# One small GpSimd write behind every row gather of a graph kernel's third pass

## The chip, the cores and the metric

The kernel runs on one core of one Trainium2 chip. The metric is the device time of one execution in microseconds (us), as the median of several timed runs. A profile is one further execution, recorded by the hardware profiler; its time stands beside its span below.

## The reference

Two graph layers follow each other over 12500 nodes with 64 features each and 400000 edges, whose edges are sorted by destination. The first layer takes a mean over the source nodes of each node's edges, twice, with tanh. The second layer is the one that the change lies in. For each edge it makes a gate from the edge's 64 attributes, multiplies it with the row of the edge's source node, and sums the products by destination node:

```python
def ssp(x):
    return jax.nn.softplus(x) - LOG2
h = node_feats_in @ Wn.T + bn
h_src = h[src]                                   # a row of 64 floats per edge
w = ssp(edge_feats @ We1.T + be1)
w = ssp(w @ We2.T + be2)
m = h_src * w
agg = jax.ops.segment_sum(m, dst, num_segments=V)
out = ssp(agg @ Wc.T + bc)
return out @ Wp.T + bp
```

Each layer ends with a residual addition and a layer norm.

## The kernel before

Three passes over the edges follow each other. Passes one and two serve the first layer (one-hot matrices that are counted, kept in HBM and used again, with gathers on line 438). A short stage then makes the rows `h` of the second layer and stores them in HBM as `t3`, 64 floats a node. Pass three, `edge_pass(second, message_pools)`, is the second layer's edge work.

Pass three works in 391 groups (NG = 390 and a shorter last one). A group is T = 8 columns of 128 edges, 1024 edges. The body stands in a hardware loop over `windows`, which runs once for these inputs; the 391 groups are written out inside it, and a scheduler orders the instructions of each engine by their dependencies.

- `Group.gather` (line 866) fills a tile `got` of 128 x 8 x 64 floats with eight indirect DMAs on GpSimd's queue (line 870), one per column of 128 edges: each reads 128 row numbers from `srcs` and fetches 128 rows of `t3`. There are eight `got` buffers, so the gathers may run eight groups ahead of the product that reads them. Completion is counted on eight semaphores in turn, so a gather also waits for the landing of the gather eight before it.
- `second` is a software pipeline of three stages: in step k it starts group k (gather, load of the attributes `att` on SP's queue at line 948, transposes `m_t` on TensorE, copy `m_at` on ScalarE, first layer at line 971), advances group k - 1 (second layer at line 965, logarithms on ScalarE at lines 932 and 933) and finishes group k - 2.
- Finishing a group is: transposes `m_b` (line 958), the product `m_m` = gate x `got` on VectorE (line 961), eight matmuls with the one-hot tile `same` into `p_sum` (line 885), and the addition of `p_sum` into a window of `acc` on VectorE (line 903, `Group.place`).

`m_m` is what waits for the eight gathers of its group, and its end is what frees the `got` buffer for the group eight later. GpSimd has no other work in pass three than the 3125 gathers and one MEMSET of `att` (line 947) in the short last group.

Of the kernel before, what the change touches and what calls it, by code (L numbers as in the profile page):

```python
# [9 lines left out]
F32 = mybir.dt.float32  # L10
# [9 lines left out]
P = 128  # L20
# [47 lines left out]
def gnn_kernel(ctx, tc, x, src, dst, ea, W_lin, b_lin, W1_agg, W1_root, b1, W2_agg, W2_root, b2,  # L68
               Wn, bn, We1, be1, We2, be2, Wc, bc, Wp, bp, out):
    nc = tc.nc  # L70
# [239 lines left out]
    def across(row, shape):  # L310
        return row.unsqueeze(1).to_broadcast(shape)
# [527 lines left out]
    big = ctx.enter_context(tc.tile_pool(name="big", bufs=1))  # L839
    cps = ctx.enter_context(tc.tile_pool(name="cps", bufs=1, space=PSUM))  # L840
    acc = big.tile([F, NA], F32, name="acc")
    base = big.tile([P, NG + 1], F32, name="base")
    base_i = big.tile([1, NG + 1], I32, name="base_i")
    steps = cps.tile([P, 512], F32, name="steps")
    nc.vector.tensor_copy(steps[:, :W], ramp[:, :W])
    e_att = ea[:NG * ET, :].rearrange("(g p t) f -> g p t f", p=P, t=T)
# [2 lines left out]
    def edge_pass(stages, pools):  # L849

        nc.vector.memset(acc, 0.0)
        nc.vector.tensor_copy(base, first)
        with ExitStack() as st:
            sb = st.enter_context(tc.tile_pool(name="esb", bufs=3))
            ps = st.enter_context(tc.tile_pool(name="eps", bufs=2, space=PSUM))
            work = pools(st)
            at = {}

            class Group:
                def __init__(self, g):
                    self.g, self.n = g, T if g < NG else TL
                    self.got = None

                def gather(self):
                    self.got = sb.tile([P, T, F], F32, name="got", bufs=8)
                    for t in range(self.n):
                        c = self.g * T + t
                        nc.gpsimd.indirect_dma_start(  # L870
                            out=self.got[:, t, :], out_offset=None, in_=t3[:, :],
                            in_offset=bass.IndirectOffsetOnAxis(ap=srcs[:, c:c + 1], axis=0))

                def compare(self):
                    n = self.n
                    self.same = sb.tile([P, T, W], F32, name="same")
                    nc.vector.tensor_tensor(  # L877
                        self.same[:, :n, :], across(steps[:, :W], [P, n, W]),
                        rel[:, self.g * T:self.g * T + n].unsqueeze(2).to_broadcast([P, n, W]),
                        op=ALU.is_equal)  # L880

                def gathered_sum(self, m):
                    self.p = ps.tile([F, W], F32, name="p_sum")
                    for t in range(self.n):
                        nc.tensor.matmul(self.p, m[:, t, :], self.same[:, t, :],  # L885
                                         start=t == 0, stop=t == self.n - 1)

                def place(self):
                    g = self.g
                    if g % 8 == 0:  # L890
                        k = min(8, NG + 1 - g)
                        loads, v = nc.values_load_multi_w_load_instructions(
                            base_i[0:1, g:g + k], engines=(mybir.EngineType.DVE,), min_val=0, max_val=NP,
                            skip_runtime_bounds_check_because="a base is a node's number, held at NP or "
                            "less where it moves, and acc has W columns more", bass_reorder=False)
                        at.update({g + i: v[i] for i in range(k)})
                        if g:
                            for load in loads:
                                tc.add_manual_dep(load.ins, at["last"].ins.name, mybir.DependencyInfo(
                                    mybir.DependencyClass.NoSync, mybir.DependencyReason.DATA),  # L900
                                    reason="in order")
                    here = acc[:, ds(at[g], W)]
                    at["last"] = nc.vector.tensor_tensor(here, self.p, here, op=ALU.add)  # L903

            with tc.For_i(0, windows, 1):
                nc.vector.tensor_copy(base_i, base[0:1, :])
                stages(work, [Group(g) for g in range(NG + 1)])
                nc.vector.tensor_scalar(base, base, float(W), float(NP), op0=ALU.add, op1=ALU.min)
                nc.vector.tensor_scalar(rel, rel, -float(W), None, op0=ALU.add)
# [13 lines left out]
    def second(work, groups):  # L923
# [15 lines left out]
        for k in range(len(groups) + 2):  # L939
# [38 lines left out]
            if old:  # L978
                old.gathered_sum(old.m)
                old.place()  # L980

    edge_pass(second, message_pools)


# [70 lines left out]
```

## Time and profile before

| | us |
|---|---|
| median of 3 timed runs | 6985.22 (6981.7 to 6987.38) |
| the profiled execution | 8350.39 |
| its span, first to last instruction | 8348.6 |
| first gather of pass three, last `acc` of it | 3376.3, 8216.9 |
| mean granted TensorE clock of the profiled execution | 0.760 |

The profiled execution is 1365 us longer than the median of the timed runs. Places in the profile are given in microseconds from the start of the span. In the rows of the profile, POOL is GpSimd, DVE is VectorE, ACT is ScalarE and PE is TensorE; a group of instructions is named by its line, engine and operation and by its output and input tiles, and the text behind an arrow names what ended the wait before it. "issue" is idle time for which nothing recorded was waited for; "remote" is a wait whose releaser the profile does not know.

### The profile page before, as it was taken

What the parts mean: (1) busy time and instruction counts of PE and PEld (TensorE: products, weight loads), DVE (VectorE), ACT (ScalarE), POOL (GpSimd) and SP (SyncE); (2) the same over time, 40 slices, a digit from 0 to 9 for tenths busy, and PEclk for the clock granted to TensorE, in tenths of its full rate; (3) what the DMA queues carried; (4) which work ended last, traced back from release to release, by engine and by line L of the source; (5) the groups of instructions that cost most, each with busy time, mean ns of one, the idle gap of its engine ahead of it and who ended that gap; (6) DMA issues with size and microseconds to landing.
All of it is one profiled execution on the core that took longest, in us unless ns stands there. A gap on an engine that the chain in (4) does not pass through costs nothing.

```text
span 8348.6 us, 77646 instructions
## 1 busy us (share of the span) xinstructions
PE 4576.7 (55%) x27549; PEld 2560.1 (31%) x27549; DVE 3612.9 (43%) x5716; ACT 2669.7 (32%) x4067; POOL 4837.1 (58%) x4741
## 2 busy tenths in 40 slices
PE   2788888853444445355445455544554554454555
PEld 1344444421221224233223233323332332232333
DVE  3687788751111114343434344434444443443335
ACT  1788888850000001122222222222222222222224
POOL 1676767626555551566666566666666666666660
PEclk9899999876666666677777777777777777777776
DMA  2565555565665675112111122221211211111110
GB/s 55 188 236 225 215 227 225 220 258 190 237 260 221 260 265 172 46 43 44 43 43 44 41 45 44 45 43 43 43 44 44 44 43 42 43 45 41 44 43 20
DMA packets 364128, 933.43 MB, mean 112 GB/s; under 512 B 135808, under 2 KB 167904, under 8 KB 363518
## 3 DMA queue, kind: packets, MB, share of 16 engines
q1 hardware_dynamic: 191951, 787.41, 25.2%
q0 software_dynamic: 151744, 131.99, 8.9%
q10 hardware_dynamic: 20015, 8.71, 0.5%
q8 instruction: 232, 3.80, 0.2%
q14 instruction: 186, 1.52, 0.1%
HBM read 581.70 MB, written 346.02 MB: 111 GB/s over the span
## 4 chain that ended last, share of the span: by engine, by line
another core or an unknown queue 20%; PE 14%; issue 10%; DVE 8%; ACT 3%; POOL 3%; DMA 2%; DVEq 1%; POOLq 0%; ACTq 0%; SPq 0%
PE m L965 5%; PE m L971 3%; POOL got L870 3%; PE p_sum L885 3%; DVE m_v L936 2%; DMA got<-t,srcs 2%; DVE m_m L961 1%; DVE same L877 1%; ACT m_w L932 1%; ACT m_at L954 1%; DVE m_w L928 1%; ACT m_w L933 1%; DVE m_v L928 1%; PE m_b L958 1%
## 5 line engine op out<-in xcount | busy, mean ns | idle before, releaser
L870 POOL DMA_INDIRECT got<-t,srcs x3125 | 2968.6, 950 | 2023.9 <-DVE m_m L961 924.1
L438 POOL DMA_INDIRECT got<-sent,gidx x1578 | 1818.8, 1153 | 1265.9 <-PE p_got L449 503.8
L965 PE MATMUL m<-m_v,we 128*128 128x512 f32 x782 | 626.6, 894 | 1991.2 <-DVE m_v L936 1714.5
L530 ACT CAST counts<-p_counts 128x784 bf16<-128x784 f32 x1664 | 1284.0, 821 | 249.7 <-PE p_counts L528 134.4
L932 ACT ACTIVATE m_w<-m_w 128x512 f32<-128x512 f32 x391 | 246.9, 631 | 3035.2 <-DVE m_w L928 2626.5
L528 PE MATMUL p_counts<-to,lo 128*128 128x392 bf16 x3328 | 882.6, 355 | 216.6 <-ACT counts L530 145.2
L885 PEld LDWEIGHTS p_sum<-same,m_m 128*64 128x64 f32 x6250 | 776.5, 153 | 535.1 <-DVE m_w L928 233.1
L885 PE MATMUL p_sum<-same,m_m 128*64 128x128 f32 x6250 | 872.9, 299 | 94.5 <-DVE m_m L961 93.0
L903 DVE TENSOR_TENSOR acc<-p_sum,acc 64x128 f32 x391 | 110.1, 282 | 1829.1 <-remote 1634.5
L515 DVE TENSOR_TENSOR to<-ramp,keys 128x1568 bf16<-128x1568 f16 x832 | 797.3, 971 | 156.9 <-PE p_counts L528 95.4
L965 PEld LDWEIGHTS m<-m_v,we 128*128 128x128 f32 x782 | 156.1, 249 | 2079.1 <-DVE m_v L936 1776.7
L674 PE MATMUL p_sums<-counts,addends 128*64 128x512 bf16 x2548 | 460.4, 463 | 237.4 <-issue 192.3
L971 PE MATMUL m<-m_at,we 128*128 128x512 f32 x782 | 570.4, 822 | 0.7 <-ACT m_at L954 0.7
L537 PE MATMUL p_sums<-counts,addends 128*64 128x256 bf16 x5096 | 487.0, 286 | 8.2 <-ACT counts L530 4.3
L877 DVE TENSOR_TENSOR same<-steps,rel 128x1024 f32<-128x1024 f32 x391 | 471.4, 1206 | 0.0
L528 PEld LDWEIGHTS <-lo 128*128 128x128 bf16 x3328 | 263.4, 102 | 586.6 <-issue 483.0
L961 DVE TENSOR_TENSOR m_m<-m_b,got 128x512 f32<-128x512 f32 x391 | 267.3, 684 | 369.9 <-remote 160.3
L681 ACT COPY rs<-p_sums 128x512 f32<-128x512 f32 x26 | 15.2, 586 | 1257.6 <-remote 1020.3
L954 ACT COPY m_at<-m_t 128x512 f32<-128x512 f32 x391 | 225.4, 576 | 595.8 <-PE m L971 481.3
L936 DVE SCALAR_TENSOR_TENSOR m_w<-m,be_c,m_w 128x512 f32<-128x512 f32 x391 | 292.7, 749 | 268.3 <-ACT m_w L933 149.9
L958 PE MATMUL m_b<-ident,m_w 128*128 128x128 f32 x1564 | 248.8, 283 | 288.4 <-DVE m_w L936 173.7
L553 DVE TENSOR_TENSOR v_rest<-misc,parts 128x68 f32<-128x68 f32 x52 | 11.8, 227 | 911.5 <-ACT parts L550 908.8
(263 smaller groups left out, 5191.4 us busy)
## 6 DMA issues: line engine op xcount, KB each, us to landing
kept<-counts SPq DMA_DIRECT2D x364, 896.0 KB
counts<-kept SPq DMA_DIRECT2D x364, 896.0 KB
att<-in_edge_attr_dram SPq DMA_DIRECT2D x390, 256.0 KB
got<-t,srcs POOLq DMA_INDIRECT x3125
got<-sent,gidx POOLq DMA_INDIRECT x1578
t<-h SPq DMA_DIRECT2D x7, 448.0 KB
xs<-in_x_dram ACTq DMA_DIRECT2D x6, 448.0 KB
xs<-in_x_dram SPq DMA_DIRECT2D x6, 448.0 KB
```

What stands on the lines that cost most here:

```text
L438: nc.gpsimd.indirect_dma_start(out=got[i][:, t, :], out_offset=None, in_=sent[step][:, :], in_offset=bass.IndirectOffsetOnAxis(ap=gidx[:, ...
L515: nc.vector.tensor_tensor(t.rearrange("p n (j two) -> p n j two", two=2), ramp[:, :width].rearrange("p (j two) -> p j two", two=2).unsquee ...
L528: nc.tensor.matmul(p[:, k, :MW], made["lo"][:, q % 4 * 2 + k, :], made["to"][:, q % 2 * 2 + k, :], start=True, stop=True)
L530: nc.scalar.copy(counts[:, :, q * 2 * DW:(q + 1) * 2 * DW].rearrange("p h (k d) -> p h k d", k=2), p[:, :, :MW].rearrange("p k (d h) -> p ...
L537: nc.tensor.matmul(p[r:r + YW, :HI * DW], addends[:, h, :], counts[:, h - of, :], start=h < 2, stop=h >= NPP - 2)
L674: nc.tensor.matmul(p[r:r + YW, :], addends[:, h, :], counts[:, :, j, :], start=h < 2, stop=h >= NPP - 2)
L870: nc.gpsimd.indirect_dma_start(out=self.got[:, t, :], out_offset=None, in_=t3[:, :], in_offset=bass.IndirectOffsetOnAxis(ap=srcs[:, c:c + ...
L877: nc.vector.tensor_tensor(self.same[:, :n, :], across(steps[:, :W], [P, n, W]), rel[:, self.g * T:self.g * T + n].unsqueeze(2).to_broadcas ...
L885: nc.tensor.matmul(self.p, m[:, t, :], self.same[:, t, :], start=t == 0, stop=t == self.n - 1)
L936: nc.vector.scalar_tensor_tensor(a, p, bias, a, op0=ALU.add, op1=ALU.max)
L965: nc.tensor.matmul(mid.p2, we2, mid.v, start=True, stop=True)
L971: nc.tensor.matmul(new.p1, we1, at, start=True, stop=True)
```

## The change

A tile `apart` of 128 x 1 floats is made beside `acc`, and behind every indirect DMA of `Group.gather` the source has one GpSimd MEMSET of zeros to it. Nothing reads the tile. Lines below line 843 move down by one or two.

```diff
     base_i = big.tile([1, NG + 1], I32, name="base_i")
+    apart = big.tile([P, 1], F32, name="apart")
     steps = cps.tile([P, 512], F32, name="steps")
...
                         nc.gpsimd.indirect_dma_start(
                             out=self.got[:, t, :], out_offset=None, in_=t3[:, :],
                             in_offset=bass.IndirectOffsetOnAxis(ap=srcs[:, c:c + 1], axis=0))
+                        nc.gpsimd.memset(apart, 0.0)
```

## The prediction

> **What bounds the kernel now.** I read the page's busy times and slices first, to find pass three; then the waits inside it; then the timelines of GpSimd and of VectorE, because the change touches one instruction stream alone.
>
> ```profile
> POOL 1676767626555551566666566666666666666660
> ...
> L870 POOL DMA_INDIRECT got<-t,srcs x3125 | 2968.6, 950 | 2023.9 <-DVE m_m L961 924.1
> ```
>
> The first is GpSimd's row of the page's 40 slices, the second a group of the page. The gathers of pass three (line 870) start at 3376.3 us, the last `acc` update is at 8216.9 us: pass three has 4841 us of the 8348.6 us span. 3125 gathers keep GpSimd busy for 2969 us at about 0.95 us each, and no slice of GpSimd is full. The waits of 3700 to 8200 us say why (total, times, longest):
>
> ```profile
> DVE acc L903 <- remote: 1535.1, 172, 13.5
> POOL got L870 <- DVE m_m L961: 877.1, 206, 7.3
> POOL got L870 <- issue: 764.3, 2491, 1.3
> ```
>
> Third row: nearly every gather begins about 0.30 us after the one before has ended, with nothing to wait for. So a gather costs 0.947 + 0.304 = 1.251 us from start to start, 10.0 us for a group of eight, and 3125 x 1.251 = 3909 us for the pass if nothing holds it up. Second row: in the profiled execution GpSimd also stands still for a `got` buffer, which `m_m` of eight groups earlier frees; it is the faster side there. First row: what holds the compute side is a stall of VectorE before `acc` that nothing recorded explains. In VectorE's timeline:
>
> ```profile
> 5013.13 0.28 DVE L903 TENSOR_TENSOR acc<-p_sum,acc 64x128 f32 x1 [11.62 <-remote]
> ...
> 5023.16 0.28 DVE L903 TENSOR_TENSOR acc<-p_sum,acc 64x128 f32 x1 [2.10 <-PE m_b L958]
> ...
> 5030.67 0.27 DVE L903 TENSOR_TENSOR acc<-p_sum,acc 64x128 f32 x1
> ```
>
> Without the stall one group takes 5030.67 - 5023.16 = 7.5 us of compute; with the stalls the mean is 4841 / 391 = 12.4 us. GpSimd's 10.0 us lie between.
>
> The timed runs decide which side counts. The profiled execution took 8350.39 us (span 8348.6, so 2 us around it), the median of the timed runs is 6985.22: 1365 us less. If pass three ran at GpSimd's pace there, it would save 4841 - 3909 = 932 us, and 433 would come from the 3376 us before it. If the stalls stayed, the whole 1365 us would have to come from those 3376, 40% of them, though TensorE is 82 to 87% busy from 200 to 1700 us (409 to 434 us of each 500 in the table of stretches). So I take the stall to belong to the profiled execution and the gathers, at 10.0 us a group against 7.5 of compute, to bound pass three in the timed runs. That is inferred, not seen.
>
> **The change part by part.** It adds 3125 writes of zero to a 128x1 tile, one in the source behind each gather; it removes nothing. In the changed program the streams of TensorE, VectorE, ScalarE and SP hold the same instructions in the same order with the same waits. Only GpSimd's differs, and not as the words say. Each write waits for the completion of the write before it (same tile, GpSimd's own semaphore), and for nothing else; the scheduler pulls the writes ahead of gathers that still wait for a buffer. The order is: 120 gathers (groups 0 to 14) with one write between any two; then 113 groups with 14 to 35 writes in a row ahead of each, mostly 25, none inside a group; then the last 2101 gathers with no write at all. In all 119 + 14 + 14 x 35 + 14 x 27 + 84 x 25 + 24 = 3125, so 3006 stand in rows.
>
> What one write costs. The trace has these on GpSimd:
>
> ```profile
> 0.25 0.10 POOL L1044 MEMSET const-float32-0.0<- 128x1 f32 x1 [0.25 <-issue]
> 0.28 0.10 POOL L1044 MEMSET const-float32-1.0<- 128x1 f32 x1
> 0.30 0.11 POOL L1044 MEMSET const-bfloat16-1.0<- 128x1 bf16 x1
> 0.33 0.12 POOL L1044 MEMSET const-uint8-127<- 128x1 uint8 x1
> 0.74 0.20 POOL masks.py:197 MEMSET ident<- 128x128 f32 x1 [0.29 <-POOLq L1044]
> ```
>
> ```profile
> 8154.50 0.95 POOL L870 DMA_INDIRECT got<-t,srcs  x1 [0.30 <-issue]
> 8155.49 0.53 POOL L947 MEMSET att<- 128x512 f32 x1
> 8156.65 0.95 POOL L870 DMA_INDIRECT got<-t,srcs  x1 [0.64 <-DVE m_m L961]
> 8157.91 0.95 POOL L870 DMA_INDIRECT got<-t,srcs  x1 [0.30 <-issue]
> ```
>
> A 128x1 write takes 0.10 us, 128x128 takes 0.20, 128x512 takes 0.53 even straight behind a gather: 0.10 fixed and 0.83 ns an element. So mixing gathers and writes makes neither longer; the 0.64 us before the next gather is put down to `m_m`, which ends at 8156.38, and the usual 0.27 us from there to a gather's start is the rest.
>
> For 3006 writes in rows two readings compete. The rows: the four constants wait for nothing and end at 0.35, 0.38, 0.42 and 0.45 us, 0.035 us apart, because the next is under way before the one ahead has completed. The Trainium skill (Perfetto Trace Analysis, section GPSIMD Engine Instruction) advises just that measure: distrust the reported span on GpSimd and use the spacing of consecutive instructions. It would price the rows at 3006 x 0.035 = 105 us. But those four have no wait between them, and the new writes have one each: completion has to be signalled first. GPSIMD Engine Reference, section Instruction dispatch, draws that line: completion does not hold back the next Pool instruction, only what waits for the semaphore. So I take the full 0.10 us, plus the 0.03 us that a single wait on an engine's own semaphore costs (0.01 from end to signal for the `ident` write, about 0.02 from signal to start on VectorE and ScalarE): 0.13 us. No chain of small GpSimd writes is in the trace; the ends I keep are 0.035 below and 0.25 above (twice the value, if the wait costs as much again as the write).
>
> Sum for the timed runs: rows 3006 x 0.13 = 391 us. Between single gathers the wait is long over; a write costs between 0.035 and 0.14 us (0.04 to its start plus 0.10), 119 x 0.09 = 11 us. Together 402 us, all on GpSimd, which I hold to be the bound: in groups 15 to 127 it needs 10.0 + 26.6 x 0.13 = 13.5 us a group against 7.5. Behind GpSimd's writes are queued the next group's gathers; who waits for them is `m_m` (line 961), then `p_sum` and `acc`. The buffer lead of eight groups covers nothing there, since a slower GpSimd has no lead. The `att` loads on SP, the port to SBUF (0.5 KB a write) and the extra 200 KB of instruction code are costed at nothing: GpSimd's own 13.5 us a group covers them, and as `att` is 256 KB a group already loaded in 7.5 to 12 us, a loss there would be below 1 us a group.
>
> Against the profiled execution's own 8350.39 us the sum is smaller: at 12.4 us a group GpSimd has slack, so groups 15 to 127 pay 113 x (13.5 - 12.4) = 123 us, less up to eight groups of lead (about 80 us): 8390 to 8475 us, if its stalls recur as before.
>
> **The rivals.** (A) GpSimd bounds the timed pass: 6985 + 402 = 7387; with 0.11 to 0.18 us a write, 7325 to 7545. For: the arithmetic of the 1365 us. Against: in the one execution that can be seen, it waits for buffers.
>
> (B) The stalls are partly real in the timed runs, and slack hides part of the writes. At 11.3 us a group, halfway, the 113 groups pay 113 x (13.5 - 11.3) = 249 us, less 80 of lead: about 7155. For: the 206 waits for `m_m`. Against: 1365 us can't be found then.
>
> (C) The wait on the own semaphore is as good as free and writes pass at 0.035 us: 105 + 4 = 109 us, 7094.
>
> (D) The other side: faster. Many stalls end 2.5 to 4 us after GpSimd's last gather, when it has run out of buffers (last gather at 4011.13 us, `acc` at 4015.08); a pause in the gathers may be what releases TensorE. The rows of writes are such a pause in front of each of 113 groups. It pays only if the timed pass is stall-bound (say 11.3 us a group) and GpSimd stays under that, so from below (11.3 - 10.0) / 26.6 = 0.049 us a write; at 0.035 it gives 113 x (11.3 - 10.9) = 45 us, 6940.
>
> (E) The change doesn't do what it says: that much is certain for 3006 of 3125 writes. Its effect is in (A); were all of it hidden, 6985.
>
> **How the numbers follow.** A 0.65, B 0.14, C 0.05, a write near 0.25 us (3006 x 0.25 = 750 us, about 7740) 0.07, E hidden 0.03, D 0.06. The time given is A's, rounded to 7385. The range has A's (up to 7545) and goes down to 7110, which takes in B and leaves out C, D and E below and the dearest writes above, some 2 in 10. Faster is D, 0.06; same is E, 0.03; slower is the rest, 0.91. About 0.2% (14 us) is what a measurement of this kernel can tell from no change.
>
> **What would show it right or wrong.** Right: about 26 MEMSETs of `apart` in a row ahead of each group from about the 121st gather on, starting 0.13 us apart; gathers still 0.947 us long and 1.251 apart inside a group; GpSimd's waits for `m_m` gone in groups 15 to 127 and back after them. Wrong: writes starting 0.035 or 0.25 us apart; a gather behind a write longer than 0.95 us, or starting more than 0.30 us after it; stalls before `acc` that go away in the groups with rows; a timed loss far below 300 us, which would say that GpSimd was not the bound of the timed pass.

## The result and the profile after

The changed kernel takes 7502.28 us (median of 4 runs, 7496.97 to 7508.05) against 6986.3 us (the three runs before and one more, 6981.7 to 6995.71): a ratio of 1.0737, 95% interval 1.0718 to 1.0755, or 516 us more. The forecast was 7385 us in a range of 7110 to 7545.

The profile of before that the prediction was read from belongs to a disturbed execution, 20% above every timed run (what disturbed it is not known); when the same kernel was profiled again, as the run before_again, that execution took 6984.9 us (span 6983.1), and after's profiled one took 7496.97 (span 7495.1). These two are compared here. First the undisturbed profile of before: GpSimd's slices, the shares of the chain that ended last, and the group of the gathers (busy us, mean ns | idle us ahead, most of it).

```profile
POOL 0787777772777774277777777777777777777771
...
POOL 32%; DMA 13%; issue 11%; PE 2%; DVE 1%; ACT 1%; POOLq 0%; another core or an unknown queue 0%; DVEq 0%; ACTq 0%; SPq 0%
...
L870 POOL DMA_INDIRECT got<-t,srcs x3125 | 2963.0, 948 | 1150.8 <-issue 839.2
```

GpSimd stands at 7 tenths through all of pass three (0.945 us of each 1.249), the chain runs through it and its transfers, and the idle time ahead of the gathers is "issue", no longer `m_m`. The waits of pass three (2917 to 6857 us; total, times, longest) say who waits for whom:

```profile
DVE m_m L961 <- DMA got<-t,srcs: 1520.4, 384, 5.0
...
POOL got L870 <- issue: 839.2, 2755, 0.3
```

VectorE waits for the gathers in 384 of 391 groups. GpSimd starts nearly every gather 0.3 us after the one before has ended, and no wait of its own for `m_m` is left. So the prediction's inference holds: pass three runs at GpSimd's pace. Now after, the same rows of its page, with the writes:

```profile
POOL 0877777736777743777677767777777777777771
...
L871 POOL DMA_INDIRECT got<-t,srcs x3125 | 2961.1, 948 | 1174.6 <-issue 898.4
...
L874 POOL MEMSET apart<- 128x1 f32 x3125 | 311.2, 100 | 167.2
```

The gathers have kept their length (948 ns). The writes hold the engine for only 311 us, with 167 us idle ahead of them. Three stretches of after's pass three show where the time went: lone writes, then rows of writes, then none.

```profile
core 0: us, PE busy (x) PEld busy (x) DVE busy (x) ACT busy (x) POOL busy (x), PEclk, DMA share, GB/s
2924.00:3090.00 166.00, 103.21 (x432) 64.19 (x433) 87.62 (x114) 47.67 (x81) 141.07 (x254) 0.81 0.25 59
3090.00:4718.00 1628.00, 807.00 (x3170) 585.73 (x3169) 546.44 (x792) 339.31 (x568) 1148.27 (x3897) 0.73 0.17 37
4718.00:7341.00 2623.00, 1692.43 (x7244) 1100.79 (x7242) 1237.05 (x1812) 773.38 (x1293) 1982.72 (x2102) 0.82 0.24 52
```

Only the middle stretch differs: 113 groups in 1628 us, 14.4 us each, where before takes 9.99. TensorE is half busy there and its granted clock drops to 0.73, but it is not what holds the groups up: `m_m` waits for the gathers in all 113 of them, 894 us in total, and TensorE's sums into `p_sum` wait for `m_m` as often. The last stretch has before's pace (1.2485 us from gather to gather). From the first to the last gather pass three takes 4415.2 us against 3914.2: 501 of the 512 us between the two spans. Another 8 lie ahead of the pass and 3 behind it; both are left unexplained.

GpSimd's timeline shows the two kinds of place (start, length, engine and line, operation, idle time ahead). Lone writes:

```profile
3083.53 0.94 POOL L871 DMA_INDIRECT got<-t,srcs  x1 [0.19 <-issue]
3084.48 0.11 POOL L874 MEMSET apart<- 128x1 f32 x1
3084.78 0.94 POOL L871 DMA_INDIRECT got<-t,srcs  x1 [0.19 <-issue]
```

The write starts as soon as the gather ends and the next gather starts 0.30 us after that same end, as it does with no write between: 3084.78 - 3083.53 = 1.25. A lone write in such a place costs nothing. And a row of 35 ahead of a group's first gather:

```profile
3098.46 0.94 POOL L871 DMA_INDIRECT got<-t,srcs  x1 [0.30 <-issue]
3099.41 5.42 POOL L874 MEMSET apart<- 128x1 f32 x35
3105.44 0.94 POOL L871 DMA_INDIRECT got<-t,srcs  x1 [0.61 <-DVE m_w L938]
3106.68 0.94 POOL L871 DMA_INDIRECT got<-t,srcs  x1 [0.30 <-issue]
```

35 writes take 5.42 us: (5.42 - 0.10) / 34 = 0.156 us from start to start, of which 0.098 is the write and 0.058 passes from its end to the next start. Behind the row the gather waits another 0.61 us, twice the usual 0.30. The profile names `m_w` as releaser, a tile that the gather does not read; the experiments say what it is.

So a row of n writes adds (n - 1) x 0.156 us, plus at its end 0.94 + 0.70 - 1.249 = 0.39 us (gather, last write's start to the gather's start, usual pitch). Over 114 rows with 3006 writes that is 2892 x 0.156 + 114 x 0.39 = 451 + 45 = 496 us, against 501 in the trace. Four of the missing five come from five late gathers of a kind that `between` shows more of, below.

### The profile page after: what moved, and what is told of

Same layout as the page of the kernel before. It is cut to its first block, busy times and chain, and to the rows that moved or that the text cites. A ratio compares the mean times of both kernels' runs of the same rounds, so it can differ in the third digit from the quotient of the medians.

```text
span 7495.1 us, 80771 instructions
## 1 busy us (share of the span) xinstructions
PE 4737.4 (63%) x27549; PEld 2859.5 (38%) x27549; DVE 3566.9 (48%) x5716; ACT 2651.1 (35%) x4067; POOL 5124.5 (68%) x7866
## 5 line engine op out<-in xcount | busy, mean ns | idle before, releaser
L887 PE MATMUL p_sum<-same,m_m 128*64 128x128 f32 x6250 | 1155.8, 362 | 1327.6 <-DVE m_m L963 1327.0
L887 PEld LDWEIGHTS p_sum<-same,m_m 128*64 128x64 f32 x6250 | 1026.7, 189 | 1712.4 <-DVE m_m L963 1708.2
L967 PE MATMUL m<-m_v,we 128*128 128x512 f32 x782 | 513.5, 743 | 292.3 <-DVE m_v L938 291.6
L449 PE MATMUL p_got<-got,same 128*128 128x51 bf16 x3156 | 218.3, 198 | 431.8 <-DMA got<-sent,gidx 401.2
L973 PE MATMUL m<-m_at,we 128*128 128x512 f32 x782 | 477.9, 698 | 0.7 <-ACT m_at L956 0.7
L874 POOL MEMSET apart<- 128x1 f32 x3125 | 311.2, 100 | 167.2
L674 PE MATMUL p_sums<-counts,addends 128*64 128x512 bf16 x2548 | 400.4, 482 | 35.4 <-DMA sent<-addends 23.0
L960 PE MATMUL m_b<-ident,m_w 128*128 128x128 f32 x1564 | 285.1, 313 | 148.2 <-DVE m_w L938 148.1
L954 PE MATMUL m_t<-ident,att 128*128 128x128 f32 x1564 | 332.9, 350 | 56.9 <-DMA att<-in_edge_attr_dram 43.7
L449 PEld LDWEIGHTS <-same 128*128 128x128 bf16 x3156 | 160.1, 104 | 524.6 <-issue 456.7
```

Source lines behind the costliest of these rows:

```text
L449: nc.tensor.matmul(p[:, k * SW:(k + 1) * SW], same[:, t, k * P:(k + 1) * P], rows[:, t, :SW], start=t == 0, stop=t == n - 1)
L674: nc.tensor.matmul(p[r:r + YW, :], addends[:, h, :], counts[:, :, j, :], start=h < 2, stop=h >= NPP - 2)
L887: nc.tensor.matmul(self.p, m[:, t, :], self.same[:, t, :], start=t == 0, stop=t == self.n - 1)
L967: nc.tensor.matmul(mid.p2, we2, mid.v, start=True, stop=True)
L973: nc.tensor.matmul(new.p1, we1, at, start=True, stop=True)
```

## The experiments

Each is the kernel before with other writes in pass three, and each gives GpSimd's instructions of pass three a fixed order: `behind` ties each to the one before it in the source, without a wait, so that no writes are pulled ahead. The diffs below show only what differs beyond this:

```diff
+                def behind(self, made):
+                    if "pool" in at:
+                        tc.add_manual_dep(made.ins, at["pool"].ins.name, mybir.DependencyInfo(
+                            mybir.DependencyClass.NoSync, mybir.DependencyReason.DATA), reason="in order")
+                    at["pool"] = made
```

The theory at the start: GpSimd bounds pass three at 1.249 us a gather; a write costs only where it is chained behind another. The rivals: that the stalls belong to the kernel; that any write between gathers costs; that the price is the write, not the wait.

### Before, profiled again

No edit.

> The kernel before, profiled once more. Theory: the stalls before acc in the first profile belong to that execution alone; an undisturbed one has its span near 6985 us, with the first gather of pass three near 2924 us (as in the profile after), gathers 1.249 us apart without a break (3125 x 1.249 = 3903 us) and no wait of GpSimd for m_m. Rival (recording this kernel brings the stalls each time, because its gathers leave no pause): again some 8350 us with 1500 us of stalls before acc.

It took 6984.9 us, with the lines shown above: pass three from 2916.10 (first gather) to 6856.28 us (last `acc`), gathers 1.249 us apart throughout, no stall ahead of `acc`. The rival falls: profiling this kernel does not bring the stalls each time. The pass starts 460 us earlier than in the disturbed profile, where the prediction had worked out 433.

### One write between any two gathers, in fact

```diff
-                        nc.gpsimd.indirect_dma_start(
+                        self.behind(nc.gpsimd.indirect_dma_start(
...
+                        self.behind(nc.gpsimd.memset(apart, 0.0))
```

> The same 3125 writes, but each held between its two gathers by an order of the program (no semaphore added), so that there is no row of writes. Theory from the 119 such places in the profile after (gather to write 0.944 us, write to gather 0.305, together the 1.249 of a gather alone): a lone write lies inside the 0.30 us that a gather takes to start, and costs nothing: 6985 us, within 15. Rivals: the step of the prediction, 0.09 us a write: 7266; a write's whole span and its start, 0.14 us: 7422; the spacing of free writes, 0.035: 7094.

7009.95 us against 6991.02, ratio 1.0028 (1.0019 to 1.0038): 3125 writes for 19 us, or 6 ns each. What the change says it does costs about 1/27 of what the changed kernel costs. The timeline has, besides the free place, a rarer one:

```profile
3188.67 0.95 POOL L877 DMA_INDIRECT got<-t,srcs  x1 [0.19 <-issue]
3189.61 0.12 POOL L880 MEMSET apart<- 128x1 f32 x1
3190.26 0.94 POOL L877 DMA_INDIRECT got<-t,srcs  x1 [0.53 <-issue]
```

The last gather starts 0.34 us late. There are 29 of these, exactly every 106th gather of the pass from the 100th on, 0.34 us late or, every fourth time, 1.13: 15 us in all, most of the 19. before_again has no late gather at these places. The same gathers, by number, are late in other kernels below, more so shortly behind chained writes: in `rows_front` 1.78 us as the second gather of a group, 0.18 as the fourth, not at all as the sixth or eighth. So what delays them goes by the count of gathers and not by time. I found nothing in the trace that they wait for; their cause is open.

### A row of eight writes ahead of each group, or inside it

The same 3125 writes, eight in a row, in two places. `rows_front`:

```diff
+                        if t == 0:
+                            for _ in range(self.n):
+                                self.behind(nc.gpsimd.memset(apart, 0.0))
                         self.behind(nc.gpsimd.indirect_dma_start(
```

> The writes of a group (8) in one row ahead of its first gather, all groups alike. Theory: in a row each write costs 0.156 us because it waits for the completion of the one before, the first lies in the gather's start, and the gather behind the row starts 0.39 us later than it would: 391 x (7 x 0.156 + 0.39) = 580 us, 7565. Rival, the step of the prediction (0.13 us for each write, nothing at the end of a row): 3125 x 0.13 = 406 us, 7391.

`rows_mid`, behind the fourth gather of a group:

```diff
                             in_offset=bass.IndirectOffsetOnAxis(ap=srcs[:, c:c + 1], axis=0)))
+                        if t == min(3, self.n - 1):
+                            for _ in range(self.n):
+                                self.behind(nc.gpsimd.memset(apart, 0.0))
```

> The same rows of 8 writes, but behind the fourth gather of each group, where the gather that follows waits for one semaphore instead of two. If the 0.39 us at the end of a row belong to the gather with two waits: 391 x 7 x 0.156 = 427 us, 7412. If they belong to any gather behind a row: 580 us, 7565, as with the row in front.

`rows_front` took 7594.32 us, ratio 1.0858 (1.0839 to 1.0876), 603 us more. `rows_mid` took 7405.44, ratio 1.0592 (1.0574 to 1.061), 414 us more. GpSimd's timeline of `rows_front`:

```profile
3217.91 0.94 POOL L880 DMA_INDIRECT got<-t,srcs  x1 [0.30 <-issue]
3218.86 1.21 POOL L879 MEMSET apart<- 128x1 f32 x8
3220.68 0.94 POOL L880 DMA_INDIRECT got<-t,srcs  x1 [0.61 <-issue]
```

and of `rows_mid`:

```profile
3212.06 0.94 POOL L877 DMA_INDIRECT got<-t,srcs  x1 [0.30 <-issue]
3212.99 1.22 POOL L882 MEMSET apart<- 128x1 f32 x8
3214.36 0.94 POOL L877 DMA_INDIRECT got<-t,srcs  x1
```

The rows are equally long. The gather behind them starts 0.61 us after the end of the last write in the first kernel and 0.15 us in the second: 0.455 us more. So the extra at a row's end belongs to the first gather of a group. That gather has two waits, one for the landing of the gather eight before and one for its `got` buffer; the others have the first alone. `rows_front` itself holds the test of this: the first eight groups use their buffer for the first time and need not wait for it, and the gathers behind the rows of groups 1 to 7 all lack the extra, while those of the 383 later groups have it. One of the seven:

```profile
2957.02 1.21 POOL L879 MEMSET apart<- 128x1 f32 x8
2958.38 0.94 POOL L880 DMA_INDIRECT got<-t,srcs  x1
```

The gather starts 0.15 us after the row's end here too. It is the second wait that costs 0.455 us: 383 x 0.455 = 174 us, where the two times differ by 189; the late gathers make 12 of the rest.

The trace records one of the two as an entry of its own in GpSimd's queue. In before_again such an entry is done at 3430.69 us for a gather that starts at 3438.31: 7.6 us ahead, and it costs nothing. In `rows_front` it is done at 3219.95, beside the start of the row's last write (3219.97), and its gather starts 0.73 us later. Over all groups the lead is 7.6 us in before_again, 5.2 in `rows_mid`, 1.4 in `between` and 0.70 in `rows_front` (medians), and only the last pays. My reading is that the queue runs ahead of the engine and so hides the entry, and that a chain of waiting writes right ahead of it takes the lead away; no run shows how the queue works inside.

The sums close. In `rows_front` the first gather of a group starts 2.753 us after the one before it instead of 1.249, or 2.30 in groups 1 to 7: 383 x 1.504 + 7 x 1.05 = 583 us, and 14 us of late gathers of `between`'s kind make 597, which is what its trace has over before_again's from first to last gather (603 by the timed runs). For `rows_mid` it is 391 x 1.047 = 409, and 409 by the traces (414 by the timed runs).

### The same row without the wait on the neighbour

Eight tiles in turn, so that a write waits only for the write of the group before, long done.

```diff
+    apart = [big.tile([P, 1], F32, name=f"apart{i}") for i in range(8)]
...
+                        if t == 0:
+                            for i in range(self.n):
+                                self.behind(nc.gpsimd.memset(apart[i], 0.0))
```

> Rows of 8 writes ahead of each group's first gather, but to eight tiles in turn, so that a write waits for the write of the group before and not for its neighbour. If the wait for the neighbour's completion is what a write in a row costs (theory), writes follow each other every 0.035 us or so: 391 x (7 x 0.035 + 0.39) = 248 us, 7233, or about 95 us (7080) if the 0.39 at the end of the row goes too. Rival: a write in a row costs 0.156 us whatever it waits for: 7565 as with one tile.

7061.2 us, ratio 1.0096 (1.0079 to 1.0113), 65 us more against the 603 of `rows_front`: same place, same number of writes, same bytes, as many instructions more. The row in GpSimd's timeline:

```profile
3187.54 0.94 POOL L880 DMA_INDIRECT got<-t,srcs  x1 [0.30 <-issue]
3188.48 0.32 POOL L879 MEMSET apart<- 128x1 f32 x8
3188.95 0.94 POOL L880 DMA_INDIRECT got<-t,srcs  x1 [0.15 <-issue]
```

Eight writes in 0.32 us: 0.028 us from start to start instead of 0.156, though each takes 0.12, and the gather follows after 0.15 us, not 0.61. Each group pays 0.162 us (391 x 0.162 = 63 of the 65). The queue entry of the second wait is 5.4 us ahead of its gather again, and there are no late gathers of `between`'s kind. Both parts of the loss thus hang on one thing, the wait of each write for the completion of the one before. This is the line that the Trainium skill draws in GPSIMD Engine Reference, section Instruction dispatch, and the traces agree with it: 0.028 us where a write waits for nothing new, 0.156 where it waits for its neighbour. Both expectations were too high: a write takes 0.028 us and not 0.035, and the gather starts 0.27 us after the start of the last write, not 0.305.

### Two chained writes between any two gathers

```diff
+                        self.behind(nc.gpsimd.memset(apart, 0.0))
+                        self.behind(nc.gpsimd.memset(apart, 0.0))
```

> Two writes to the one tile between any two gathers, the second waiting for the first. Theory: the first is hidden, the second comes 0.156 us later and pushes the gather's start by as much: 3125 x 0.156 = 487 us, 7472. Rival (whatever fits into the 0.30 us of a gather's start is hidden; two writes end 0.27 us after the gather): no change, 6985. What the profile is to show: how long after the last write the next gather starts.

7553.71 us, ratio 1.0802 (1.078 to 1.0824), 557 us more. Neither number was met. GpSimd's timeline inside a group, and (last row) ahead of a group's first gather:

```profile
3121.86 0.12 POOL L880 MEMSET apart<- 128x1 f32 x1
3122.03 0.10 POOL L881 MEMSET apart<- 128x1 f32 x1
3122.28 0.94 POOL L877 DMA_INDIRECT got<-t,srcs  x1
...
3125.46 0.94 POOL L877 DMA_INDIRECT got<-t,srcs  x1 [0.60 <-issue]
```

Inside a group the second write starts 0.17 us after the first and the gather 0.15 us after its end: 0.42 us from the gather's end instead of 0.305, so +0.112. The group's first gather, with its two waits, shows 0.60 us again and pays 0.565, except in groups 1 to 7, where it pays what the others do; the lead of the queue entry is 0.70 us, as in `rows_front`. Together 0.112 x 2741 + 0.565 x 383 = 307 + 216 = 523 us. The 29 late gathers of `between` stand here too, 1.48 us late or, every fourth time, 1.73, 45 us in all: 568, where the traces differ by 572 from first to last gather (557 by the timed runs). One write a gather costs 19 us, a second one behind it 538 more.

### How long a lone write may be

One write between any two gathers, as in `between`, of 32, 128 and 256 columns. The edit is the tile:

```diff
-    apart = big.tile([P, 1], F32, name="apart")
+    apart = big.tile([P, 256], F32, name="apart")
```

> One write between any two gathers, of 128x256 instead of 128x1: 0.31 us instead of 0.10. If a gather's start comes 0.19 us behind the end of the write ahead of it (as behind the lone 128x1 write), the pitch is 0.944 + 0.31 + 0.19 = 1.45 us: 3125 x 0.20 = 620 us, 7605. Rival: a gather's start runs beside the write, as it is prepared elsewhere than the writes are made, and the pitch is the longer of the two, 1.25 to 1.26 us: within 40 us of 6985.

256 columns: 7605.39 us, ratio 1.0876 (1.0854 to 1.0898), 609 us more. From its timeline, with the write and the gather behind it:

```profile
3225.53 0.34 POOL L880 MEMSET apart<- 128x256 f32 x1
3226.03 0.95 POOL L877 DMA_INDIRECT got<-t,srcs  x1 [0.16 <-issue]
```

The gather starts 0.165 us after the write's end, 0.49 after the gather before. From this and `two_between` I formed a rule: a gather starts 0.305 us after the gather before or about 0.15 to 0.165 after the end of the write ahead, whichever is later, so about 0.15 us of write is free. 32 and 128 columns were run to test it on either side of that point:

```diff
+    apart = big.tile([P, 32], F32, name="apart")
```

> One write between any two gathers, of 128x32. Theory formed from the runs so far: a gather starts at the later of two times, 0.305 us behind the end of the gather ahead and about 0.155 us behind the end of the write ahead. A 128x32 write ends 0.14 us behind the gather: 0.14 + 0.155 = 0.295 us, still below 0.305, so nothing is added to the kernel with the 128x1 write (7010). Rival (a write's length beyond 128x1 always shows): 31 elements x 0.83 ns x 3125 = 80 us more, 7090.

```diff
+    apart = big.tile([P, 128], F32, name="apart")
```

> The same with 128x128: the write ends 0.225 us behind the gather, plus 0.155 is 0.38 us, 0.075 above 0.305: 3125 x 0.075 = 234 us over the kernel with the 128x1 write, 7245. Rivals: the length beyond 128x1 shows in full, 127 x 0.83 ns x 3125 = 330 us, 7340; a gather's start runs beside the write, no change.

32 columns: 7037.46 us, ratio 1.0061 (1.0044 to 1.0077), 44 us more. 128 columns: 7281.32 us, ratio 1.041 (1.0392 to 1.0427), 288 us more. Timeline of the first:

```profile
3226.01 0.15 POOL L880 MEMSET apart<- 128x32 f32 x1
3226.32 0.95 POOL L877 DMA_INDIRECT got<-t,srcs  x1 [0.17 <-issue]
```

and of the second:

```profile
3226.13 0.22 POOL L880 MEMSET apart<- 128x128 f32 x1
3226.52 0.95 POOL L877 DMA_INDIRECT got<-t,srcs  x1 [0.17 <-issue]
```

With 32 columns the gather still starts 0.31 us after the write's start: the length is hidden. With 128 it starts 0.384 us after the end of the gather before, as the rule has it (0.22 + 0.165). The rule is right on the starts, and the times lie 27 and 36 us above what it gave. The traces put most of that elsewhere: the gathers themselves take 0.950 us with 32, 128 and 256 columns instead of 0.945 (medians; some 17 us over 3125), the pass begins some 10 us later than in `between`, and with 128 columns the gather starts 0.384 us after the one before and not 0.380, another 12 us. Why a gather grows by 5 or 6 ns was not found.

| writes in pass three | us more | what a write adds |
|---|---|---|
| one between, 128x1 | 19 | nothing in its place |
| one between, 128x32 | 44 | nothing in its place |
| one between, 128x128 | 288 | 0.085 us, 0.006 of it the longer gather |
| one between, 128x256 | 609 | 0.192 us, 0.006 of it the longer gather |
| two between, chained | 557 | 0.112 us a pair, 0.565 at a group's start |
| rows of 8 ahead, each to its own tile | 65 | 0.028 us in a row |
| rows of 8 inside, one tile | 414 | 0.156 us in a row |
| rows of 8 ahead, one tile | 603 | 0.156 us, and 0.455 at the end of a row |

## Why the prediction was right, and where it was off

Right:

- **The bound.** GpSimd was inferred from the 1365 us that the profiled execution had too many; before_again shows it (no wait for `m_m`, 1.249 us a gather), and `between` against `rows_front` moves the time by GpSimd's own delays alone.
- **The order.** Writes in rows ahead of 113 groups, and none among the last 2101 gathers, came from the instruction streams; the three stretches of after are these parts. after's trace has these rows to the last write: 84 of 25, 14 of 27, 14 of 35, one of 14, one of 24. Taken from the words of the change, the kernel to price would have been `between`, which loses 19 us, and 281 by the prediction's own 0.09 us a lone write.
- **The wait, not the write.** Of the prediction's two prices for a row, 0.035 us by the spacing of the four constants and 0.13 with a wait, the runs have both: 0.028 without the chain, 0.156 with it. The spacing that Perfetto Trace Analysis (GPSIMD Engine Instruction) in the Trainium skill advises was the right measure, taken on rows that had no chain; rival C falls because the new rows have one.
- **The gathers** kept their length in after, as it said.

Off, in the terms of its sum of 402 us:

- **The wait on the own semaphore** was the mis-sized term: 0.03 us was taken, 0.058 is what passes from a write's end to the next start. In after's trace the signal comes 0.011 us after the end, as it was taken from the `ident` write (0.01); the start comes 0.047 us after the signal, where 0.02 was taken from VectorE and ScalarE. The step from signal to start on another engine was no measure for GpSimd's. 0.026 us a write more over 2892 writes: +75 us.
- **The end of a row** was set at the usual 0.30 us and takes 0.61, because the gather there has two waits; from the row's last write on that is 0.39 us a row more than a gather alone: 114 x 0.39 = +45 us. The prediction named "a gather starting more than 0.30 us after it" as a sign against itself; it is there.
- **The first write of a row and the lone writes** were charged and are free, beneath the 0.305 us to the next gather: -114 x 0.13 = -15 and -11 us.
- Together 402 + 75 + 45 - 15 - 11 = 496, and 4 us of late gathers make the 501 of the trace but for 1. The rest to 516 is the 11 us ahead of and behind the pass, and run-to-run spread. The terms put at nothing (`att` loads, port, code) left nothing to find: `rows_front_free` has as many writes and as much more code, and pays 65 us, 63 of which are its rows.
- **The profiled execution after**, forecast at 8390 to 8475 us "if its stalls recur", took 7497: they did not recur. The `m_m` waits are not "back after" the rows either: before_again has none, and after one, of 0.6 us.

The other rivals: B and D both need stalls in the timed pass, and before_again, an execution as long as the timed ones, has none. D also needs writes below 0.049 us; `rows_front_free` has these, at 0.028, and is 65 us slower. E was true of what the change does (3006 of 3125 writes are not between two gathers), and it is what makes it cost 516 us and not 19.

No kernel here is faster than the one before: each only adds work.

## What to carry to other kernels

An instruction that nobody reads is not placed by its line in the source: look at the engine's stream before pricing it, and fix the order if the place matters. On a bound engine, the number of instructions said little here and the chains between them nearly everything: the same 3125 writes cost 19, 65, 414 or 603 us, by whether each waits for the one before and by what stands behind the row. And where one profiled execution lies far from the timed runs, take it again before trusting its waits; the arithmetic between the two gave the right bound, but showed none of it.

## What the runs showed of the hardware

- GpSimd's small writes (128x1) overlap: 0.028 us from start to start with each 0.12 long (`rows_front_free`). One that waits for the completion of the one before starts 0.058 us after its end, 0.011 to the signal and 0.047 from there: 0.156 from start to start (after).
- Between two row gathers of 128 rows GpSimd has 0.305 us in which another instruction is free, as long as it ends about 0.15 us before the next gather is due: 128x32 still fits, 128x128 does not.
- A second wait of a gather is a queue entry of its own. It cost nothing in the plain stream, where it was done 7.6 us ahead (before_again), and 0.455 us behind a chain of writes waiting for each other, where the lead was 0.70 us (`rows_front`; the seven gathers there without the second wait pay nothing).
- Every 106th gather starts late where chained writes stand shortly ahead of it (0.34 us or 1.13 in `between`), and not in before_again or `rows_front_free`. The cause is not known.
